# A four-layer decoder on one core: order of the first layers' softmax, of the last context keys and of the first 32-head queries

## Chip, core and metric

The kernel runs on one NeuronCore of a Trainium2 chip as a single program. The metric is the device time of one execution, in microseconds (us); lower is better. All work is in that one launch: eight sub-layers, one after another, on 1024 rows of 512 values.

## What is computed

`x` is (16, 64, 512) and is handled as 1024 rows in 8 tiles of 128 rows. `ctx` is a context of the same shape. Each of four layers adds a cross attention and a feed-forward to `x`:

```
x = x + L0_xattn(layernorm(x), ctx)   # 8 heads, a window of 16 places along the 512 columns, rows as channels
x = x + L0_ffn(layernorm(x))          # int8 fake-quantised gate, up, down; silu; clip
x = x + L1_xattn(layernorm(x), ctx)   # 32 query heads, 8 key heads of 128, keys and queries RMS-normed
x = x + L1_ffn(layernorm(x))          # mxfp4 fake-quantised weight and input
x = x + L2_xattn(layernorm(x), ctx, ctx)  # 32 query heads of 16
x = x + L2_ffn(layernorm(x))          # 16 of 64 low-rank experts per row
x = x + L3_xattn(layernorm(x), ctx)   # 16 query heads of 96
x = x + L3_ffn(layernorm(x))          # 3-bit weight
```

In L0, every place of the 512 columns attends to 16 neighbouring places: the scores of a tile are 16 x 16 x 512 values, a softmax over the 16, and a weighted sum of 16 shifted copies of the values. In L1 the keys and values come from `concat([context, latents])`, so half of them depend on the context alone and can be made before L0 is done.

## The kernel before

**Two lanes on one instruction stream.** Every sub-layer is a Python generator that issues instructions and yields an estimated cost of what it has issued. `merged` (L1840) runs two of them: `main` and `side`. After each step of `main`, with cost c, it advances `side` until the costs that `side` has yielded reach `rate` x c. `side` marks its progress with `MARK`; `main` asks for it with `Need(n, rate)`: `merged` then advances `side` alone, with nothing of `main` between, until more than n marks have come, and goes on with the new rate. TensorE (PE) takes its instructions exactly in the order in which they are traced (`tc.manual_schedule(engines={PE})`, L1975). The other engines and the SyncE queue (SP), which issues all DMAs, are ordered by the framework's scheduler from trace order and its own estimates; `behind_main` and `issue_after` pin a DVE instruction behind the last DVE instruction that `main` has traced.

**What runs when.** `side` does L0 for the four groups of two tiles each (window attention, then the int8 feed-forward), and yields a `MARK` after each group's feed-forward. After that it does L1_ffn to the end of the decoder for the first four tiles. `main` does L1's attention: first the context keys and values of all 32 units (4 pairs of key heads x 8 tiles), then for each group of two tiles 8 key heads x 2 tiles, and afterwards L1_ffn to the end for the last four tiles.

**Window attention** (`WindowAttention`, L231). `__init__` loads its weights `w4` and biases `bcol`; `context` loads a context tile `cn`; `normed` makes the layernorm; `keys_values` and `queries` make the padded keys `kp`, values `vp` and `qs` (PE tiles ps_kv0 and ps_q0, line L323); `dots` multiplies shifted keys with queries on DVE (`prod`, L371), sums over the head's rows on PE (L392), copies the result to `dots`, and turns it with a round trip through DRAM (`dots_d`, L402 and L404). `softmax` (L409) works on two halves of a tile: maximum and subtraction on DVE (L420, L421), exponential on ACT (L422), sum and reciprocal on DVE (L426, L427), product on GpSimd (POOL, L428), and yields 1.5 after the exponential and 1.5 after the product, so 6 in all for a tile. The weights go to DRAM (`att_d`, L431) and come back spread out (`att`, `load`, L443: four buffers). `output` (L448) multiplies them with the values on DVE (`pv`, L468, pinned behind main's last DVE instruction) and adds the products up on POOL (`acc`, L478): 16 steps, each of two products and two additions. `project` multiplies with the output weights on PE (L323).

**Int8 feed-forward** (`Int8Ffn`, L515). Its weights come through a staging tile `room` of 128 x 1024 in three parts: `load` (L538, SP) and `split` (L546 on ACT and L547 on POOL: a high part and the rest). `load(n+1)` overwrites `room` and so waits for `split(n)`. `load_rows` (L556) then loads six rows of scales, spread over all partitions, into `rv` (128 x 2304). `steps` runs a tile through norm, scale, turn, hidden (PE ps_gu, L615), gated, limited, turn_hidden, down (PE ps_dn, L652; `y` L660, `x` L661), and then `normed.norm` and `normed.turn` make the next layernorm of the tile and transpose it (PE ps_xT, copied on ACT L178) into `kvT`, from which L1 makes its queries.

**Context keys in L1** (`normed_attention`, L752). `context_keys` multiplies a context tile with the weights of a key-head pair (PE ps_ckv, L812; 16 matmuls), copies the result on ACT (`ckv`, L821), squares it (`csq`, L823) and makes the RMS factor `r` (DVE L801, L802; POOL L125). Two units later `context_scale` multiplies the keys by it (`ckn`, L831, in the two buffers of tag `qn`), and four units later `context_turn` transposes them (PE ps_ckT), scales the copy (ACT L837) and saves keys and values to DRAM (`s`, L839). The costs are 3.4, 0.0 and 0.3. All 32 units finish, with the four turns that trail, before `Need(2, 0.85)` and the first queries:

```
        pair_weights(0)
        yield Need(1, 0.95)
        yield from ticks(
            [(hp, t) for hp in range(NKV // 2) for ts in groups for t in ts],
            [(4, context_turn, 0.3), (2, context_scale, 0.0), (0, context_keys, 3.4)],
        )
```

**The units of L1's attention** follow: per unit `queries` (PE ps_q, L860, and the loads of the saved `kT` and `v`; `v` has six buffers), `keys_values` (PE ps_kv, L878), `scale`, `turn`, `scores`, `turn_weights`, `values`, `project` with costs that add up to 11.4; a group has 16 units.

**Block sums** (`block_sums`, L1234). For L2_ffn and L3_xattn the weights are combined once on POOL (L1258, four subtractions for each of 14 parts, two buffers) and stored to DRAM (`sums_d`, L1247). They are traced while `side` is in `small_head_attention`, one subtraction after four out of five of its steps; `store(n - 1)` is traced in the third subtraction of part n.

## Time and profile before

| what | value |
|---|---|
| median of 3 runs | 1616.03 us (1613.99 to 1616.12) |
| the profiled execution | 1613.3 us, of which the span is 1611.5 us |
| PE (matmuls) busy | 1552.4 us, 96% of the span |
| DVE, POOL, ACT busy | 1006.4, 629.2, 624.9 us |
| DMA | 226.49 MB, mean 141 GB/s |

Two rows of the page show the span in 40 slices of 40.3 us, in tenths:

```profile
PE   7899899999999999999999999999999999999999
...
PEclk9999899999999999999999999999999999999999
DMA  7992349623694346954436932214211005231031
```

How to read it: a digit 9 means 90% or more. PE is below that in the first slice, in the second to third and in the fifth; there the granted clock of TensorE is lower, too. DMA is near its full share in the second and third slice. In the views by instruction, a line has the start, the time, the engine with its line, operation and tiles, how many there are, and in brackets the engine's idle time before it with what ended that.

### The profile page before, as it was taken

To read this page: it belongs to the slowest core of one execution; us is meant where nothing else is said; L and a number is where in the kernel's file an instruction comes from. 1 tells how busy PE (TensorE), PEld (TensorE's weight loads), DVE (VectorE), ACT (ScalarE), POOL (GpSimd) and SP (SyncE) were. 2 spreads that over 40 slices of the span, in tenths; PEclk is the share of its full clock that TensorE was granted. 3 is DMA by queue.
4 is the path that set the end of the run, shared out by engine and by line. 5 is a ranking of instruction groups with operands and counts; after the bars stand their busy time and mean duration, and the time that the engine had idled before them with its cause. 6 is when DMAs were issued, how large, how long until landed. Compare 5 with 4: busy or idle time off the path is not lost.

```text
span 1611.5 us, 21995 instructions
## 1 busy us (share of the span) xinstructions
PE 1552.4 (96%) x7446; PEld 976.8 (61%) x7446; DVE 1006.4 (62%) x2133; ACT 624.9 (39%) x1951; POOL 629.2 (39%) x666
## 2 busy tenths in 40 slices
PE   7899899999999999999999999999999999999999
PEld 2234456565555655566665566577666688866886
DVE  7687488676697566777954265358535564822445
ACT  3333444334443444344443354321235533213451
POOL 2394237632385313853325643234113233311232
PEclk9999899999999999999999999999999999999999
DMA  7992349623694346954436932214211005231031
GB/s 235 275 282 89 113 140 283 194 88 119 188 277 135 119 140 179 260 171 175 157 133 213 319 136 74 98 46 179 96 46 47 1 27 190 57 119 41 24 118 40
DMA packets 108703, 226.49 MB, mean 141 GB/s; under 512 B 50096, under 2 KB 67632, under 8 KB 97968
## 3 DMA queue, kind: packets, MB, share of 16 engines
q1 hardware_dynamic: 108592, 225.09, 44.3%
q8 instruction: 60, 0.98, 0.2%
q14 instruction: 51, 0.42, 0.1%
HBM read 198.32 MB, written 26.74 MB: 140 GB/s over the span
## 4 chain that ended last, share of the span: by engine, by line
PE 70%; DVE 12%; DMA 7%; POOL 4%; ACT 3%; issue 3%; SPq 0%; ACTq 0%; POOLq 0%; DVEq 0%
PE ps_wo L746 9%; PE ps_q L860 9%; PE ps_q L1674 5%; PE ps_kv L878 5%; PE ps_s L696 4%; PE ps_wo L1285 4%; PE ps_a L737 4%; PE ps_ckv L812 3%; PE ps_pT L143 3%; PE ps_k L1658 3%; PE ps_v L1616 3%; PE ps_h L1285 3%; DMA sums_d<-sums 2%; PE ps_o L1285 2%; DMA att<-att_d 2%
## 5 line engine op out<-in xcount | busy, mean ns | idle before, releaser
L746 PE MATMUL ps_wo<-l1a_o,aT 128*128 128x512 f32 x512 | 232.9, 598 | 3.3 <-ACT aT L930 3.1
L860 PE MATMUL ps_q<-l1a_w,kvT 128*128 128x512 f32 x512 | 232.7, 597 | 0.0
L712 ACT ACTIVATE p<-ps_s,mx 128x128 f32<-128x128 f32 x384 | 135.7, 370 | 218.2 <-DVE mx L707 195.1
L721 POOL TENSOR_TENSOR p<-p,sm 128x512 f32<-128x512 f32 x96 | 104.0, 1084 | 238.3 <-DVE sm L720 210.6
L125 POOL TENSOR_TENSOR r<-r,mhalf 128x5 f32<-128x5 f32 (+1 forms) x96 | 102.0, 1062 | 216.3 <-DVE r L802 213.1
L860 PEld LDWEIGHTS ps_q<-l1a_w,kvT 128*128 128x128 f32 x512 | 96.2, 191 | 116.6 <-issue 115.0
L746 PEld LDWEIGHTS ps_wo<-l1a_o,aT 128*128 128x128 f32 x512 | 93.2, 192 | 101.3 <-issue 96.3
L878 PE MATMUL ps_kv<-l1a_w,kvT 128*128 128x256 f32 x512 | 122.3, 382 | 2.4 <-DVE x L159 2.4
L478 POOL TENSOR_TENSOR acc<-acc,pv 128x512 f32<-128x512 f32 x96 | 122.1, 1296 | 3.7 <-DVE pv L468 3.0
L812 PE MATMUL ps_ckv<-l1a_kv,kvT 128*64 128x512 f32 x512 | 116.9, 598 | 5.1 <-ACT ckv L821 5.1
L801 DVE TENSOR_REDUCE r<-sq 128x5 f32<-128x640 f32 x64 | 52.2, 816 | 101.2 <-ACT sq L886 101.1
L878 PEld LDWEIGHTS ps_kv<-l1a_w,kvT 128*128 128x128 f32 x512 | 92.5, 190 | 17.8 <-DVE x L159 3.8
L125 POOL TENSOR_TENSOR rs<-rs,mhalf 128x1 f32<-128x1 f32 x64 | 37.9, 601 | 153.1 <-DVE rs L134 142.8
L868 ACT ACTIVATE sq<-ps_q 128x512 f32<-128x512 f32 x64 | 38.3, 598 | 152.3 <-PE ps_q L860 152.3
L468 DVE TENSOR_TENSOR pv<-att,ps_v 128x512 f32<-128x512 f32 x128 | 82.0, 676 | 23.1 <-DMA att<-att_d 20.8
L696 PE MATMUL ps_s<-kT,qT 128*128 128x128 f32 (+1 forms) x704 | 91.7, 276 | 0.1
L371 DVE TENSOR_TENSOR prod<-qs,kp 128x1024 f32<-128x1024 f32 x64 | 80.8, 1300 | 13.8 <-ACT qs L352 6.9
L159 DVE TENSOR_TENSOR x<-x,ps_wo 128x512 f32<-128x512 f32 x76 | 51.3, 675 | 57.5 <-PE ps_wo L1206 35.1
L696 PEld LDWEIGHTS ps_s<-kT,qT 128*128 128x128 f32 (+1 forms) x704 | 85.1, 192 | 2.5 <-issue 0.9
L1674 PE MATMUL ps_q<-kvT,l3a_w 128*128 128x256 f32 x384 | 85.5, 379 | 0.0
L728 DVE COPY pT<-ps_pT 128x512 f32<-128x512 f32 x96 | 64.3, 681 | 28.9 <-PE ps_pT L143 28.8
L712 ACT ACTIVATION_READ_ACCUMULATOR p<-ps_s,mx 128x1 f32 x384 | 79.9, 208 | 0.0
(231 smaller groups left out, 2968.1 us busy)
## 6 DMA issues: line engine op xcount, KB each, us to landing
l1a_w<-in_l1a_w SPq DMA_DIRECT2D x32, 1536.0 KB, 7.2
att<-att_d SPq DMA_DIRECT2D x64, 512.0 KB, 8.8
l1a_o<-in_l1a_w SPq DMA_DIRECT2D x32, 1024.0 KB, 5.3
w_sums<-sums_d SPq DMA_DIRECT2D x28, 512.0 KB, 5.5
w_sums<-in_sums_w SPq DMA_DIRECT2D x28, 384.0 KB, 4.4
s<-ckv SPq DMA_DIRECT2D x32, 256.0 KB, 4.7
raw<-in_sums_w SPq DMA_DIRECT2D x14, 512.0 KB, 4.6
sums_d<-sums SPq DMA_DIRECT2D x14, 512.0 KB, 5.9
```

The lines of the kernel that those rows point to most:

```text
L125: self.nc.gpsimd.tensor_tensor(out, v, self.k.mhalf[:, : v.shape[1]], ALU.pow)
L468: nc.vector.tensor_tensor(pv.rearrange("p (q w n) -> p q w n", w=2, n=L), att[:, a, :].rearrange("p (q w n) -> p q w n", w=2, n=L), spaced ...
L478: nc.gpsimd.tensor_tensor(sums, before, pv, ALU.add)
L696: nc.tensor.matmul(ps[:, i, :], lhsT=qT[:, i // 2, 2 * (i % 2) : 2 * (i % 2) + 2, :].rearrange("p g s -> p (g s)"), rhs=kTs[i // 2], start ...
L712: nc.scalar.activation(p[:, i, :], ps[:, i, :], AF.Exp, bias=mx[:, i : i + 1], scale=self.scale, accum_out=sm[:, i : i + 1],)
L721: nc.gpsimd.tensor_tensor(p, p, bc(sm, 2, P), ALU.mult)
L746: self.nc.tensor.matmul(ps, lhsT=a, rhs=wo[:, g, :], start=g == 0, stop=g == len(chunks) - 1)
L812: nc.tensor.matmul(ps[j * S : (j + 1) * S], lhsT=k.context(c, 2 * t + 1 - j), rhs=w_pair[hp][:, c, :], start=c == 0, stop=c == NC - 1,)
L860: nc.tensor.matmul(ps, lhsT=k.stream(c, t), rhs=w_qkv[n][0][:, c, :], start=c == 0, stop=c == NC - 1,)
L878: nc.tensor.matmul(ps, lhsT=k.stream(c, t), rhs=w_qkv[n][1][:, c, :], start=c == 0, stop=c == NC - 1,)
L1285: self.ln.nc.tensor.matmul(ps[:, i % 2], lhsT=a(e), rhs=w[:, b * W2 : (b + 1) * W2], start=e == 0, stop=e == len(self.rhs) - 1,)
L1674: nc.tensor.matmul(ps[:, j], lhsT=wq[:, c, (j0 + j) * P : (j0 + j + 1) * P], rhs=k.kvT[:, c, t : t + 2, 1:3, :], start=c == 0, stop=c == N ...
```

## The change

The diff does these things:

- `w4`, `bcol` and the context tiles 0 and 1 are loaded from ACT's queue and no longer from SP's.
- `softmax` is cut into `shifted` (maximum, subtraction), `raised` (exponential) and `divided` (sum, reciprocal, product). The exponential of a half is traced one step after its subtraction, together with the other half's `shifted`. The yields are 3.0, 3.0, 1.5 and 1.5: 9 for a tile.
- `room` is now the first 1024 columns of `rv`, so `load_rows` waits for the last `split`.
- For the first group `Int8Ffn` is run with `last_apart`: the second tile's `normed.turn` is left out of the list of steps. The `MARK` comes at the end of `steps`, and after it a yield of 4.0, the second tile's turn and a yield of 1.0.
- `context_scale` puts `ckn` into tag `v` (six buffers).
- The context steps run, at rate 1.08 in place of 0.95, until the last `context_keys` and one step more. The five steps that remain are taken by `rest(2)` at the end of each `queries` and `keys_values`.
- The rates of the four groups are 0.9, 0.815, 0.815, 0.775 in place of 0.85, 0.78, 0.78, 0.74.
- `block_sums` traces `store(n - 1)` in the second subtraction, and is advanced by one step for every 1.4 of cost that `small_head_attention` yields.

```diff
@@ WindowAttention.__init__
-        nc.sync.dma_start(self.w4, wt)
+        nc.scalar.dma_start(self.w4, wt)
...
-        nc.sync.dma_start(self.bcol, bias)
+        nc.scalar.dma_start(self.bcol, bias)
@@ WindowAttention.context
-        self.ln.nc.sync.dma_start(cn, self.ctx_in[t * P : (t + 1) * P, :])
+        queue = self.ln.nc.scalar if t < 2 else self.ln.nc.sync
+        queue.dma_start(cn, self.ctx_in[t * P : (t + 1) * P, :])
@@ WindowAttention.softmax
-        for c in range(2):
-            part = e[:, :, c * n_at_once : (c + 1) * n_at_once]
-            by_place = part.rearrange("p w n -> p n w")
+        parts = [e[:, :, c * n_at_once : (c + 1) * n_at_once] for c in range(2)]
+
+        def shifted(part):
             mx = ln.small.tile([P, n_at_once], F32, tag="mx0", name="mx0")
             with ln.behind_main():
-                nc.vector.tensor_reduce(mx, by_place, AX.X, ALU.max)
+                nc.vector.tensor_reduce(mx, part.rearrange("p w n -> p n w"), AX.X, ALU.max)
                 nc.vector.tensor_tensor(part, part, bc(mx, 1, WIN), ALU.subtract)
+
+        def raised(part):
             nc.scalar.activation(part, part, AF.Exp, scale=8.0**-0.5)
-            yield 1.5
+
+        def divided(part):
             sm = ln.small.tile([P, n_at_once], F32, tag="sm0", name="sm0")
             with ln.behind_main():
-                nc.vector.tensor_reduce(sm, by_place, AX.X, ALU.add)
+                nc.vector.tensor_reduce(sm, part.rearrange("p w n -> p n w"), AX.X, ALU.add)
                 nc.vector.reciprocal(sm, sm)
             nc.gpsimd.tensor_tensor(part, part, bc(sm, 1, WIN), ALU.mult)
-            yield 1.5
+
+        shifted(parts[0])
+        yield 3.0
+        raised(parts[0])
+        shifted(parts[1])
+        yield 3.0
+        raised(parts[1])
+        divided(parts[0])
+        yield 1.5
+        divided(parts[1])
+        yield 1.5
@@ Int8Ffn.__init__
-        self.room = pool.tile([P, 1024], F32, tag="room", name="room")
         self.rv = pool.tile([P, sum(r.shape[0] for r in rows)], F32, tag="rv", name="rv")
+        self.room = self.rv[:, 0:1024]
@@ Int8Ffn.steps
+        def turn_out(t):
+            if not (last_apart and t == tiles[-1]):
+                normed.turn(t)
...
-                (6, normed.turn, 1.0),
+                (6, turn_out, 1.0),
...
+        yield MARK
+        if last_apart:
+            yield 4.0
+            normed.turn(tiles[-1])
+            yield 1.0
@@ normed_attention
-            kn = pool.tile([P, G, HD], F32, tag="qn", name="ckn")[:, 0:2, :]
+            kn = pool.tile([P, 2, HD], F32, tag="v", name="ckn", bufs=6)
...
+            rest(2)
...
-        yield Need(1, 0.95)
-        yield from ticks(
-            [(hp, t) for hp in range(NKV // 2) for ts in groups for t in ts],
+        yield Need(1, 1.08)
+        units = [(hp, t) for hp in range(NKV // 2) for ts in groups for t in ts]
+        context = ticks(
+            units,
             [(4, context_turn, 0.3), (2, context_scale, 0.0), (0, context_keys, 3.4)],
         )
+        while units[-1] not in kept:
+            yield next(context)
+        yield next(context)
+
+        def rest(n):
+            for _ in range(n):
+                next(context, None)
@@ block_sums
-            if out == 2:
+            if out == 1:
                 store(n - 1)
@@ first_layers
-                yield from ffn.run(tiles)
-                yield MARK
+                yield from ffn.run(tiles, n == 0)
@@ side
-            for n, cost in enumerate(small_head_attention(b, halves[0], i["l2a_w"], weights)):
-                if n % 5 < 4:
+            spent = 0.0
+            for cost in small_head_attention(b, halves[0], i["l2a_w"], weights):
+                spent += cost
+                while spent > 1.4:
                     next(sums, None)
+                    spent -= 1.4
@@ main
-            a, groups, [0.85, 0.78, 0.78, 0.74], i["l1a_w"], i["l1a_kv"], i["l1a_n"]
+            a, groups, [0.9, 0.815, 0.815, 0.775], i["l1a_w"], i["l1a_kv"], i["l1a_n"]
```

More of the change, by code (lines that the diff above doesn't have):

```diff
@@ L558, in load_rows, with run, steps @@
             at += n
-    def run(self, tiles):
+    def run(self, tiles, last_apart=False):
         with ExitStack() as es:
-            yield from self.steps(tiles, self.ln.pool(es, "l0f"))
-    def steps(self, tiles, pool):
+            yield from self.steps(tiles, self.ln.pool(es, "l0f"), last_apart)
+    def steps(self, tiles, pool, last_apart):
         ln, k, nc = self.ln, self.ln.k, self.ln.nc
@@ L894, in keys_values @@
             d.update(kn=kn, r=r)
+            rest(2)
         def scale(u):
```

## The prediction

> **What bounds it now.** I read the busy time by stage first. PE is busy in 1552 of 1611.5 us, so nearly everything is paced by the order in which PE gets its work, and an edit that adds or removes no matmul can only win or lose PE's gaps and its slow clock. Columns: PE, PEld, DVE, ACT, POOL busy, granted clock, DMA share, GB/s.
>
> ```profile
> 40.00:80.00 40.00, 35.77 (x164) 11.35 (x162) 26.70 (x47) 14.52 (x32) 15.71 (x16) 1.00 0.91 273
> 80.00:120.00 40.00, 39.16 (x180) 12.45 (x178) 33.63 (x54) 11.45 (x28) 36.58 (x33) 1.00 1.00 282
> 120.00:160.00 40.00, 38.96 (x210) 16.17 (x208) 31.03 (x76) 15.31 (x34) 19.73 (x24) 1.00 0.29 96
> 160.00:200.00 40.00, 32.90 (x136) 16.76 (x134) 19.38 (x44) 16.24 (x43) 10.75 (x21) 0.83 0.32 114
> 200.00:240.00 40.00, 40.00 (x191) 22.44 (x188) 34.43 (x50) 19.31 (x65) 13.39 (x10) 1.00 0.44 136
> ```
>
> The reader should see the two stages where PE is short (40 to 80, 160 to 200), the clock of 0.83, and that between them POOL (36.6 of 40) and DMA (1.00) are full. PE's timeline names the gaps:
>
> ```profile
> 6.60 3.38 PE L323 MATMUL ps_kv<-cn,w 64*64 64x512 f32 x16 [6.60 <-DMA cn<-in_ctx]
> ...
> 55.28 3.65 PE L812 MATMUL ps_ckv<-l1a_kv,kvT 128*64 128x512 f32 x16 [1.41 <-ACT ckv L821]
> ...
> 60.73 3.65 PE L812 MATMUL ps_ckv<-l1a_kv,kvT 128*64 128x512 f32 x16 [1.42 <-ACT ckv L821]
> ...
> 66.15 3.65 PE L812 MATMUL ps_ckv<-l1a_kv,kvT 128*64 128x512 f32 x16 [1.40 <-ACT ckv L821]
> ...
> 126.06 1.95 PE L323 MATMUL ps_o<-acc,w 64*64 64x512 f32 x16
> ...
> 166.56 0.66 PE L143 MATMUL ps_ckT<-ident,ckn 128*128 128x128 f32 x2 [2.12 <-DVE r L802]
> ...
> 176.22 1.11 PE L143 MATMUL ps_xT<-ident,xn 128*128 128x128 f32 x4 [4.59 <-DVE rs L134]
> 177.12 5.14 PE L860 MATMUL ps_q<-l1a_w,kvT 128*128 128x512 f32 x8
> ...
> 183.82 3.60 PE L860 MATMUL ps_q<-l1a_w,kvT 128*128 128x512 f32 x8
> ```
>
> Why ACT is late three times is on its own timeline: the exponential (L422) stands first in its queue and waits 3.65 us for the subtraction, and the copy that empties PE's bank stands behind it.
>
> ```profile
> 54.13 0.63 ACT L422 ACTIVATE dots<-dots 128x512 f32<-128x512 f32 x1 [3.65 <-DVE dots L421]
> 54.66 0.57 ACT L821 COPY ckv<-ps_ckv 128x512 f32<-128x512 f32 x1
> ```
>
> Last come POOL's chain of additions, which ends 0.3 us before the output projection at 126.06, and later, among all waits, POOL's for the stored block sums:
>
> ```profile
> 74.26 1.53 POOL L478 TENSOR_TENSOR acc<-pv 128x512 f32<-128x512 f32 x1 [1.02 <-DVE pv L468]
> ...
> 124.49 1.27 POOL L478 TENSOR_TENSOR acc<-acc,pv 128x512 f32<-128x512 f32 x1
> ```
> ```profile
> POOL sums L1258 <- DMA sums_d<-sums: 18.4, 11, 2.7
> ```
>
> **The change, part by part.** Times are against the profiled execution, 1613.3 us.
>
> *Start.* Four issues leave SP: w4 0.42, bcol 0.43, two cn 0.91, together 1.76 us (SP's timeline); ACT issues them at about the same price, and is idle to 5.88. What stands behind them on SP comes as much earlier. The first matmul waits for cn, so the gain lies between 0 (DMA share is 1.08 from 4 to 8 us, the engines may be the limit) and 1.76; I take the middle, **-0.9**. [...] No run here shows two queues yet.
>
> *Exponentials.* With a step between subtraction and exponential the copy no longer stands behind a wait: 1.41 + 1.42 + 1.40 = **-4.2** (bounds 0, if the scheduler orders ACT as before, and -4.2).
>
> *Order.* Costs give where PE meets the first projection. Before, 15 (dots) + 12 (softmax) + 8 + 43.5 (output) + 5.5 = 84 of side's cost lie between the second mark and it, and main's n-th context unit has supplied 0.95 x (3.4n + 0.3(n-4)): the projection follows unit 25. After, it is 90 against 1.08 times the same: unit 23. Units follow each other in 3.96 us (70.10, 74.06). PE is therefore there at 126.06 - 0.9 - 4.2 - 2 x 3.96 = 113.0. The two units aren't lost; they now fill the feed-forward behind it.
>
> *What is late next: POOL's additions.* The first pv stands behind the r of unit 11 (72.22, then 72.30), so it moves with PE by 5.1, and the first addition from 74.3 to 69.2. From there POOL has 28 additions of 1.32 and 12 r of 0.70: 45.4 us, an end at 114.6 if POOL never waits. If the stage keeps its length (125.8 - 74.3 = 51.5, because DMA is full) it ends at 120.7. I take 116.5, two us of waiting, nearer to POOL's own rows because the first weights are stored some 7 us earlier (two halves no longer cost 5.4 us each), which moves the first loads into a stretch where DMA had room (share 0.48 from 52 to 56). The wait at the projection is **+3.5** (bounds +1.6 and +7.7). Waits of about 2 us have cost a slow clock in one place (322 to 330, granted 0.79, 1.7 us lost) and not in another (514 to 522, 2.89 us of waiting, 1.00): **+0.9**, between 0 and 1.7. [...]
>
> *The end of the first group.* Side's cost to the third mark was 124 against a supply of 112.5, so 9 to 11 units ran with nothing of main between; now 130 against 1.08 x 117.5 = 126.9, about 3. From one tile's down to its transposed layernorm takes 5.45 us (170.77 to 176.22). In the new order PE has, after the first tile's down, 2 context units, the other tile's down and three short transposes, 9.6 us; after the second's down one unit, the first's turn, the first queries and keys (3.44 + 1.73) and three short transposes, some 10.8. Both cover 5.45; without that cover the 4.59 is back. Gone are 2.12 + 0.30 + 4.59 = 7.0 and the slow clock: down 2.07 for 1.20, two xT 0.45 each, the first queries 5.14 for 3.60, 3.3 in all. New is a wait of the first queries for the first tile's copy, 0.6 as such a wait costs at 881 (0.67). **-9.7**, bounds -10.3 and -5.
>
> *Moved without a price.* The five trailing context steps are the same matmuls, copies and three stores on SP (some 0.4 each), taken between the first queries; kT and v of those heads are needed six heads later. ckn in six buffers rather than two removes a DVE wait (2.42 at 42.13) that PE does not see. The row loads of rv wait for the last split (POOL, to 46.96; they went at 40.71): on SP, stores and att loads stand behind them. The rows are first read at 132; SP may be held 6 us, hidden as long as the second tile's dots still load before their new turn, at most 2.5 us on the additions, in the bounds above.
>
> *Groups two to four.* The same counting of costs puts their projections where they were (distance from first stored weights within 1.2 us). The wait of 0.59 at 246.83, behind an exponential, goes: **-0.6**. Between turn and hidden two tiles lose their filler: about 4.4 us each (a wait of 2.06 now, at 323.59, with 2.3 of filler), against 2.06 + 2.89 today, so 3.9 more if nothing else gives; I take **+2.0** (0 to +5.6, with a slow clock).
>
> *Block sums.* 61 steps over 85.7 of cost, instead of bunched between 857 and 932. PE waits there at 924.72, 926.61 and 930.23 (1.81 + 1.15 + 1.62 = 4.58), behind an r of POOL that stands behind those sums. Earlier stores have three steps to land. **-3.5**, bounds -4.6 and +3: the moved subtractions (0.73 each) could delay POOL where it is idle now.
>
> *Rates.* Main's four groups supply 182.4 x (3.305 - 3.15) = 28.3 more, side has 23 more: it ends some 5 units ahead, and main's tail alone is 5 longer. That tail has 4.7 us of gaps in its last 112: 0, within 2.
>
> Sum: -0.9 - 4.2 + 3.5 + 0.9 - 9.7 - 0.6 + 2.0 - 3.5 = **-12.5**. The profiled execution lies 2.7 under the median shown, so 1616.0 - 12.5 = **1603.5 us**.
>
> **Rivals.**
> 1. *DMA holds the output stage at its length* (share 1.00 from 80 to 120 speaks for it, POOL's 92% against): a wait of 7.7 with a slow clock, +4.2 + 0.8 on the sum, -7.5: 1608.5. Chance 0.20.
> 2. *Nothing comes back*: no wait at the projection, none added at hidden, all of the sums: -0.9 - 4.2 - 9.7 - 0.6 - 4.6 = -20: 1596. The full POOL speaks against. 0.12.
> 3. *It doesn't do what it says.* Only PE's order is fixed; if the scheduler places exponentials and sums as before, the 4.2 stays, PE reaches the projection at 117.2 and waits to 124.9 with a slow clock: -0.9 + 7.7 + 1.7 - 9.7 + 2 = +0.8: 1617. The explicit step of cost speaks against. 0.11.
> 4. *Slower: SP is held by the row loads.* They wait for the last split, which stands on ACT and POOL among exponentials and products; att_d and att stand behind. From the store (57.87) to the first pv are 14.4 us, 2 to the first addition, then 51.5: with SP released at T the additions end at T + 68. All gain is gone when that is 128 (113 + 15 of savings), T = 60, and each us beyond costs one; at T = 65, 1621. The split ended at 46.96 and would have to slip by 13. 0.09.
>
> **Numbers.** My forecast has 0.48. Range 1594 to 1614: it takes in rivals 1 and 2 and the forecast's own bounds, and leaves out the tails and most of 3 and 4. About 0.2%, 3.2 us, is what a measurement of this kernel tells from no change: faster (under 1612.8) 0.80, same 0.09, slower 0.11.
>
> **What would show it.** Right: no bracket at ps_ckv with ACT ckv between 50 and 70; a bracket with POOL acc at the first projection, near 113, of 2 to 5 us; first queries near 166 at 3.6; clock 1.00 where 0.60 was (165 to 182); sums spread to about 1030. Wrong: a gap at the projection of 8 or more, first row loads holding SP past 50 with att behind, new brackets at ps_gu over 4, or POOL r waits new between 940 and 1040.

## The result and the profile after

| | before | after |
|---|---|---|
| median, measured together | 1616.07 us (1611.72 to 1623.32, 8 runs) | 1627.9 us (1621.44 to 1631.54, 8 runs) |
| profiled execution, its span | 1613.3, 1611.5 us | 1627.3, 1625.5 us |
| PE busy in it | 1552.4 us | 1556.5 us |
| first 32-head queries (ps_q) at | 177.12 us | 173.34 us |
| queries of unit 56, of unit 58 at | 919.32, 950.35 us | 919.85, 963.17 us |

The ratio of the times, after to before, is 1.0066 (95%: 1.0041 to 1.0091): slower by 0.7%, where 12.5 us less was forecast, and outside the range. Units are counted from 0. Of the 14 us by which the profiled executions differ, 12.3 arise between unit 56 and unit 58 of L1's attention (43.3 us for two units, before 31.0).

The busy time by stage of the changed kernel, columns as in the prediction's first table, and below them the row of the kernel before for 900 to 950:

```profile
40.00:80.00 40.00, 40.00 (x184) 12.73 (x184) 26.53 (x54) 16.04 (x35) 19.33 (x19) 1.00 0.96 290
80.00:120.00 40.00, 37.20 (x168) 11.54 (x164) 34.21 (x54) 12.42 (x29) 37.48 (x35) 1.00 0.86 267
120.00:160.00 40.00, 36.73 (x182) 16.08 (x184) 28.81 (x70) 12.22 (x26) 14.00 (x18) 0.91 0.19 66
160.00:200.00 40.00, 37.88 (x174) 19.68 (x171) 19.31 (x45) 19.12 (x51) 11.65 (x22) 1.00 0.40 137
900.00:950.00 50.00, 37.08 (x187) 21.12 (x186) 13.54 (x27) 12.64 (x40) 32.78 (x44) 0.90 0.85 282
...
900.00:950.00 50.00, 45.27 (x288) 26.88 (x287) 28.00 (x61) 20.64 (x63) 30.79 (x38) 1.00 0.74 266
```

The two stages that were short, 40 to 80 and 160 to 200, are repaired: PE is busy 40.00 us for 35.77 and 37.88 for 32.90, and the second has a clock of 1.00 for 0.83 (it is the fifth slice of the page of before, the only one there with a lower clock digit). But the stages between have lost 4.2 of the 9.2 that these won (80 to 160: 73.9, before 78.1), and 900 to 950 is new: PE 37.08 (before 45.27) at a granted clock of 0.90 (before 1.00). PE's timeline names the waits:

```profile
116.13 1.07 PE L324 MATMUL ps_o<-acc,w 64*64 64x512 f32 x2
121.06 3.56 PE L324 MATMUL ps_o<-acc,w 64*64 64x512 f32 x14 [3.85 <-POOL acc L492]
...
134.74 1.97 PE L143 MATMUL ps_q<-ident,xs 128*128 128x128 f32 x8 [2.21 <-DVE xs L597]
...
949.13 1.09 PE L143 MATMUL ps_qT<-ident,qn 128*128 128x128 f32 x4 [12.92 <-DVE sm L1208]
```

The 12.92 us are put down to the last DVE instruction to end before the matmul (`sm`). But PE's transpose reads `qn`. On DVE that stands just ahead, and waits for POOL:

```profile
928.96 0.17 DVE L825 TENSOR_SCALAR r<-r 128x5 f32<-128x5 f32 x1
...
948.29 0.69 DVE L926 TENSOR_TENSOR qn<-qn,r 128x512 f32<-128x512 f32 x1 [17.01 <-POOL r L125]
```

And this is POOL in those 18 us:

```profile
928.35 1.42 POOL L1292 TENSOR_TENSOR sums<-raw 128x256 f32<-128x256 f32 x2 [3.52 <-DMA sums_d<-sums]
929.72 1.54 POOL L1292 TENSOR_TENSOR sums<-raw,sums 128x256 f32<-128x256 f32 x2
934.78 1.41 POOL L1292 TENSOR_TENSOR sums<-raw 128x256 f32<-128x256 f32 x2 [3.52 <-DMA sums_d<-sums]
936.15 1.52 POOL L1292 TENSOR_TENSOR sums<-raw,sums 128x256 f32<-128x256 f32 x2
937.63 1.41 POOL L1292 TENSOR_TENSOR sums<-raw 128x256 f32<-128x256 f32 x2
939.00 1.52 POOL L1292 TENSOR_TENSOR sums<-raw,sums 128x256 f32<-128x256 f32 x2
943.25 1.41 POOL L1292 TENSOR_TENSOR sums<-raw 128x256 f32<-128x256 f32 x2 [2.73 <-DMA sums_d<-sums]
944.61 1.52 POOL L1292 TENSOR_TENSOR sums<-raw,sums 128x256 f32<-128x256 f32 x2
946.09 1.04 POOL L1209 TENSOR_TENSOR p<-p,sm 128x512 f32<-128x512 f32 x1
947.09 1.17 POOL L125 TENSOR_TENSOR r<-r,mhalf 128x5 f32<-128x5 f32 x1
```

The input of `r` is ready at 929.1. POOL's queue has four parts of block sums ahead of it, 16 subtractions of 0.7 us, and three of the parts wait for a stored part to leave its buffer (3.52, 3.52, 2.73; the first of these waits is over before 929.1). `r`, needed by PE, runs 18 us after it could. The sums were not spread to 1030 as forecast; the last ends at 946. They stand in one heap, as before, only a worse one. In the kernel before, `r` came behind the heap, too, but PE waited less for it:

```profile
921.19 1.53 POOL L1258 TENSOR_TENSOR sums<-raw,sums 128x256 f32<-128x256 f32 x2
922.68 1.17 POOL L125 TENSOR_TENSOR r<-r,mhalf 128x5 f32<-128x5 f32 x1
...
923.88 0.69 DVE L901 TENSOR_TENSOR qn<-qn,r 128x512 f32<-128x512 f32 x1 [5.84 <-POOL r L125]
...
924.72 0.63 PE L143 MATMUL ps_qT<-ident,qn 128*128 128x128 f32 x4 [1.81 <-DVE qn L901]
```

### The profile page after: what moved, and what is told of

Same layout as the page of the kernel before. It is cut to its first block, busy times and chain, and to the rows that moved or that the text cites. A ratio compares the mean times of both kernels' runs of the same rounds, so it can differ in the third digit from the quotient of the medians.

```text
span 1625.5 us, 21983 instructions
## 1 busy us (share of the span) xinstructions
PE 1556.5 (96%) x7442; PEld 979.6 (60%) x7446; DVE 1014.7 (62%) x2133; ACT 626.8 (39%) x1951; POOL 629.0 (39%) x666
## 4 chain that ended last, share of the span: by engine, by line
PE 74%; DVE 12%; DMA 6%; POOL 3%; ACT 2%; issue 2%; ACTq 0%; SPq 0%; DVEq 0%; POOLq 0%
PE ps_wo L769 10%; PE ps_q L883 10%; PE ps_kv L902 6%; PE ps_q L1708 5%; PE ps_s L719 4%; PE ps_a L760 4%; PE ps_wo L1319 4%; DMA att<-att_d 3%; PE ps_pT L143 3%; PE ps_ckv L835 3%; PE ps_v L1650 3%; PE ps_k L1692 3%; PE ps_h L1319 2%; PE ps_wo L1240 2%; PE ps_q L1172 2%; PE ps_o L1616 2%
## 5 line engine op out<-in xcount | busy, mean ns | idle before, releaser
L902 PE MATMUL ps_kv<-l1a_w,kvT 128*128 128x256 f32 x512 | 127.3, 393 | 5.3 <-DVE x L159 4.7
```

Source lines behind the costliest of these rows:

```text
L902: nc.tensor.matmul(ps, lhsT=k.stream(c, t), rhs=w_qkv[n][1][:, c, :], start=c == 0, stop=c == NC - 1,)
```

## The experiments

Each was timed in five rounds against the kernel before. The ratio to before is of the times; waits and positions are from one profiled execution of each, which lies up to 7 us off that kernel's median (the kernel before with both edits of the sums: 1612.6, median 1619.5).

**Which part of the block sums it was.** Four kernels. *Both edits of the sums undone:*

```diff
-            if out == 1:
+            if out == 2:
...
-            spent = 0.0
-            for cost in small_head_attention(b, halves[0], i["l2a_w"], weights):
-                spent += cost
-                while spent > 1.4:
+            for n, cost in enumerate(small_head_attention(b, halves[0], i["l2a_w"], weights)):
+                if n % 5 < 4:
                     next(sums, None)
-                    spent -= 1.4
```

> The changed kernel with the two edits of the block sums undone (one subtraction after four of five steps, store in the third subtraction). The changed kernel has one PE gap of 12.9 us at 949.13 behind an r of POOL that stands behind sums; before, there were 4.6 us of gaps at 924 to 931. H1, the edits of the sums put four parts of sums ahead of main's r: the gap falls back to 3 to 6 us, the granted clock from 900 to 950 back to 1.00, and the time is 11 to 15 below the changed kernel's 1627.9, so 1613 to 1617. H2, the shift of main against side by the new rates and the longer softmax makes the coincidence, whatever the pacing: the gap stays at 8 or more and the time above 1622. H3, the edits of the first layer cost the time: the first queries come later than 173 and the time stays above 1622 though the gap is gone.

*The kernel before with both edits alone* (the same diff the other way round):

> The kernel before with the two edits of the block sums alone. H1: a gap of 8 or more behind an r of POOL between 920 and 960, and 1624 to 1632 (8 to 15 over 1616.1). H2, the edits are harmless by themselves and only meet main's r at the new rates: gaps of 5 or less there and 1614 to 1618. My forecast's step, that the sums are spread to about 1030 and the gaps go: 1612 to 1613.

*The changed kernel, with POOL's order pinned* (`merged` keeps main's last POOL instruction as it does the last one on DVE):

```diff
-            nc.gpsimd.tensor_tensor(t[out], v, w, ALU.subtract)
+            with ln.behind_main_pool():
+                nc.gpsimd.tensor_tensor(t[out], v, w, ALU.subtract)
@@
+    def behind_main_pool(self):
+        last = self.k.last_pool_of_main
+        return self.tc.issue_after(last) if last is not None else ExitStack()
```

> The changed kernel, with every subtraction of the block sums held behind the last POOL instruction that main has traced, so that POOL takes them in traced order relative to main's r. H1 and its mechanism (POOL's order is the scheduler's own, and it takes sums ahead of the r that is traced earlier): no PE gap over 3 us between 900 and 1000, clock 1.00, sums spread from about 880 to 1030, and 1611 to 1616. H2: POOL is simply too full there and the delay returns at another r: 1620 or more.

*The pacing alone undone* (the second hunk of the first diff), the earlier store kept:

> The changed kernel with the old pacing of the block sums (one subtraction after four of five steps), but the new place of the store (second subtraction). With both edits undone the two units from 919 on took 34.4 us, with both kept 43.3, with the sums pinned 25.9, and the times were 1.0020, 1.0066 and 0.9975 of before. If the pacing made the loss, the two units take 33 to 36 us and the ratio is 1.001 to 1.003; if the earlier store made it, 41 or more and 1.005 or more.

With the kernel before and the pin (further below), they make a table; the time for two units runs from the queries of unit 56 to those of unit 58:

| kernel | two units, us | ratio to before (95%) |
|---|---|---|
| before | 31.0 | 1 |
| before, both edits of the sums | 33.4 | 1.0017 (0.9998 to 1.0036) |
| after | 43.3 | 1.0066 (1.0041 to 1.0091) |
| after, both undone | 34.4 | 1.0020 (1.0005 to 1.0035) |
| after, pacing undone | 33.8 | 1.0020 (1.0000 to 1.0040) |
| after, sums pinned | 25.9 | 0.9975 (0.9952 to 0.9997) |
| before, sums pinned | 25.3 | 0.9964 (0.9947 to 0.9981) |

The pinned kernel's POOL takes the sums in between main's work:

```profile
928.19 1.17 POOL L126 TENSOR_TENSOR r<-r,mhalf 128x5 f32<-128x5 f32 x1
929.33 0.72 POOL L1299 TENSOR_TENSOR sums<-raw,sums 128x256 f32<-128x256 f32 x1
930.01 1.17 POOL L1299 TENSOR_TENSOR sums<-raw 128x256 f32<-128x256 f32 x1
931.14 1.04 POOL L1215 TENSOR_TENSOR p<-p,sm 128x512 f32<-128x512 f32 x1
```

and its stage has no gap and no slow clock:

```profile
900.00:950.00 50.00, 50.00 (x309) 30.49 (x308) 28.46 (x57) 23.02 (x68) 26.12 (x31) 1.00 0.67 234
```

So the mechanism is shown: the loss is POOL's order, which is not that of the trace, and holding each subtraction behind main's last POOL instruction removes all of it (43.3 to 25.9 us; 1611.3 against a before of 1615.9). The heap costs the two units 5.7 us before (31.0 against 25.3) and 17.4 after. The pacing makes the larger part of the difference, the earlier store none that can be seen. My expectation that the old sums alone would give back 13 us failed: they gave back some 7 (1.0066 to 1.0020), because main's r and the heap still meet (4.25 us of waiting there and 1.18 at the next matmul; with the pacing alone undone 3.80 and 0.97). On the kernel before, the new edits cost 2.4 us in the two units, in the changed kernel 8.9. So the loss seems to need both, the pacing and the shifted lanes. That rests on one profiled execution of each: in the times the two effects are 2.7 and 7.4 us, and their difference lies within its uncertainty.

**What the rest of the change is worth.** *The kernel before, with the pin alone:*

> The kernel before, with every subtraction of the block sums held behind main's last traced POOL instruction, and nothing else. The changed kernel with the same pin ran in 1611.3. T1, the pin alone makes that time and the rest of the change nets nothing: the three gaps of before at 924 to 931 (4.6 us) go, and 1609.5 to 1612.5. T2, the pin only repairs what the new pacing broke, and the edits of the first layers are worth the 4 to 5 us by which the first queries come earlier: 1614.5 to 1617.

0.9964, against 0.9975 for the changed kernel with the pin: the rest of the change nets +0.0011, with an uncertainty of about 0.0028, or +2 us give or take 4.5. By the ratios T1 is right. Where it goes is seen in PE's idle time by stage (us, from the windows, stage less PE busy):

| kernel | 0-40 | 40-80 | 80-200 | 200-700 | 700-900 | 900-1000 | 1000-1500 |
|---|---|---|---|---|---|---|---|
| before | 8.9 | 4.2 | 9.0 | 12.7 | 3.0 | 5.4 | 11.7 |
| before, pin | 8.6 | 4.2 | 8.5 | 15.5 | 3.2 | 0.7 | 12.5 |
| after | 9.2 | 0.0 | 8.2 | 11.6 | 7.4 | 14.3 | 14.2 |
| after, pin | 9.7 | 0.0 | 9.0 | 10.3 | 7.5 | 0.7 | 14.5 |
| after, pin, old exponentials | 9.7 | 0.0 | 7.1 | 14.0 | 7.4 | 0.7 | 13.7 |
| after, pin, old end | 9.1 | 0.4 | 15.1 | 10.1 | 3.7 | 0.4 | 25.7 |
| after, pin, rates halfway | 9.5 | 0.0 | 9.5 | 12.7 | 6.8 | 1.1 | 23.3 |
| before, pin, new rates | 9.2 | 5.0 | 8.1 | 22.4 | 2.9 | 1.0 | 22.8 |
| before, pin, new end, rates 0.01 up | 9.0 | 3.8 | 8.0 | 12.6 | 1.4 | 0.1 | 25.2 |
| after, pin, both edits at the projection | 9.1 | 0.6 | 5.6 | 11.3 | 7.0 | 0.7 | 13.6 |

**The exponentials.** The old order, at the new costs:

```diff
+        for c in range(2):
...
+            nc.scalar.activation(part, part, AF.Exp, scale=8.0**-0.5)
+            yield 3.0
...
+            nc.gpsimd.tensor_tensor(part, part, bc(sm, 1, WIN), ALU.mult)
+            yield 1.5
```

> The changed kernel with the pinned sums, and the old order inside the softmax: each half's exponential directly behind its subtraction, with costs 3.0 and 1.5 for a half, so that the sum of a tile stays 9 and PE's order the same. My forecast's term: three waits of ps_ckv for ACT's ckv of 1.4 us come back between 50 and 70, and the time is 4.2 over that of the changed kernel with pinned sums, 1615.5. Rival: the additions of POOL set when the first projection runs (121 us), and whatever PE gains before, it waits there (3.8 us): the waits come back, the wait at the projection shrinks by as much, the first queries move by less than 1.5 us and the time by less than 1.5: 1610 to 1613.

1608.1, ratio 0.9943 (0.9925 to 0.9962): 5 us under the same kernel with the new order, with 5 us of uncertainty, and no row shows where they would come from (the two profiled executions are 1609.0 and 1608.8). Neither side of the expectation was right, for in this execution the three waits did not come back at all. ACT in that kernel:

```profile
52.03 0.63 ACT L429 ACTIVATE dots<-dots 128x512 f32<-128x512 f32 x1 [2.59 <-DVE dots L428]
52.57 0.57 ACT L837 COPY ckv<-ps_ckv 128x512 f32<-128x512 f32 x1
...
57.51 0.63 ACT L429 ACTIVATE dots<-dots 128x512 f32<-128x512 f32 x1 [3.69 <-DVE dots L428]
58.05 0.57 ACT L837 COPY ckv<-ps_ckv 128x512 f32<-128x512 f32 x1
...
62.97 0.63 ACT L429 ACTIVATE dots<-dots 128x512 f32<-128x512 f32 x1 [3.68 <-DVE dots L428]
63.51 0.57 ACT L837 COPY ckv<-ps_ckv 128x512 f32<-128x512 f32 x1
64.65 0.58 ACT L837 COPY ckv<-ps_ckv 128x512 f32<-128x512 f32 x1
```

The copies still stand behind the exponential's wait, and PE has no wait. A round with an exponential takes 5.5 us where PE's unit takes 3.96, so each puts ACT some 1.5 us further behind; the copy is 0.5 late at 52.57 and 3.5 at 63.51, and the second copy at 64.65 catches up. Copies up to 3.5 late left PE without a wait here. Before, the copy at 49.23 was 3.6 late already, and PE was held from 55.28 on for three rounds running.

In other kernels with the old order and the new costs, further below, a part of these waits is there, at most in the one whose first loads are on SP's queue (0.62 and then):

```profile
64.60 3.65 PE L827 MATMUL ps_ckv<-l1a_kv,kvT 128*64 128x512 f32 x16 [1.43 <-ACT ckv L836]
```

Before, PE's waits behind an exponential there add up to 4.23 us; with the old order at the new costs they are 0 to 2.05 in six kernels, and with the new order 0 to 0.82 in seven. So the step between subtraction and exponential is worth little of the 4.2. The larger part is where costs and rate together put the exponentials among main's units; no run has one without the other (old order, old costs and a rate of 1.03 leave 1.12). The step also costs: the first addition on POOL starts at 74.48 in the changed kernel, and at 72.09 and 72.21 in two kernels that have the new costs and the new end with the old order.

**The start.** *Old sums, SP's queue* and *pinned sums, old exponentials, SP's queue*:

```diff
-        nc.scalar.dma_start(self.w4, wt)
+        nc.sync.dma_start(self.w4, wt)
```

(and so for bcol and the context tiles)

> As the first of these kernels (old block sums), and with w4, bcol and the context tiles 0 and 1 loaded from SP's queue again. In the changed kernel the first matmul starts at 6.69 (before 6.60) and the first statistics of x at 4.51 (before 3.41). H1, the second queue only lets the context tiles' transfers take the place of x's: the first matmul stays within 0.2 of 6.6, x's first statistics fall back to about 3.4, the first queries come 0.5 to 1.5 earlier than in the first of these kernels, and the time is 0.5 to 1.5 lower. H2, my forecast's term: the time is 0.9 higher. H3: no difference, within 0.3.

> The same base (ratio 0.994), with w4, bcol and the context tiles 0 and 1 on SP's queue again. My forecast's start term: first matmul some 0.9 later and ratio 0.0006 higher. Theory from the executions so far (first matmul at 6.7 to 7.1 with ACT's queue in six kernels, 6.2 to 7.4 without in four): the second queue gains nothing, first matmul at 6.2 to 6.9, first statistics of x near 3.4 in place of 4.5, and a ratio of 0.992 to 0.995.

1.0026 (1.0009 to 1.0043) against 1.0020, and 0.9952 (0.9930 to 0.9974) against 0.9943. Both differences have the sign and about the size of the forecast's 0.9 us (0.0006), but lie inside uncertainties of 0.0023 and 0.0029: no gain is shown, and one of 0.9 is not excluded. The first matmul begins, over the profiled executions, at 6.7 to 7.1 with ACT's queue and at 6.2 to 7.4 without. What the two queues do shift is x: its first statistics on DVE start at 4.51 to 4.61 with ACT's queue (three profiles) and at 3.41 and 3.44 without (two), so about 1 us later.

**The end of the first group.** Undone in the changed kernel with the pin, and done without the change's other parts in the kernel before with the pin (there with rates of its own: 1.03 for the context, then 0.86, 0.79, 0.79, 0.75):

```diff
-            rest(2)
...
-        yield Need(1, 1.08)
+        yield Need(1, 0.95)
...
-        while units[-1] not in kept:
...
-                yield from ffn.run(tiles, n == 0)
+                yield from ffn.run(tiles, False)
```

> The changed kernel with the pinned sums, and the old end of the first group: no turn kept apart, all context keys and turns before the first queries, rate 0.95. My forecast's term of 9.7 for this part, less the 2.6 to 4.4 that the wait at the projection took back: the gaps of 2.1 and 4.6 and the slow clock between 160 and 182 come back, first queries at 175 to 178 instead of 171.7, and 1615 to 1620. Rival T1, that what is gained before the first queries is lost again at the later feed-forwards: first queries late as above, but the time within 1.5 of 1611.3.

> The kernel before with the pinned sums and the new end of the first group alone: second tile's turn apart, the last context steps between the first queries, ckn in six buffers; rate 1.03 for the context, and 0.86, 0.79, 0.79, 0.75 behind it, a little over the old ones. The old exponentials and costs, SP for all loads. My forecast's term for this part: no gaps of 2.1 and 4.6 and no slow clock between 160 and 182, less a wait of 3 to 5 at the first projection, which comes two units earlier: first queries 4 to 7 before 176.7, and as much off the ratio of 0.996, so 0.992 to 0.994. Rival, all of it is given back by waits behind it: first queries as early, ratio 0.995 or more.

Undone: first queries at 185.24 in place of 171.66, and 160 to 200 has 11.1 us of idle and a granted clock of 0.74. Of the 13.6 us, 8 are a later projection (129.8 for 121.7), which the lower rate brings with the longer costs. Done on the kernel before: first queries at 174.57 (before, pin: 176.70), and 34.8 us of idle up to 1000 in place of 40.7. Up to there it is a gain. But both kernels are slow, 1.0095 (1.0068 to 1.0121) and 1.0061 (1.0042 to 1.0080), and both have 25 us of idle from 1000 to 1500, where main and side are in the last layers.

**The rates.** Halfway back in the changed kernel with the pin (0.88, 0.80, 0.80, 0.76), the new ones in the kernel before with the pin, and a little up from the new ones (0.91, 0.82, 0.82, 0.78) on the version with the old exponentials:

```diff
-            a, groups, [0.9, 0.815, 0.815, 0.775], i["l1a_w"], i["l1a_kv"], i["l1a_n"]
+            a, groups, [0.88, 0.80, 0.80, 0.76], i["l1a_w"], i["l1a_kv"], i["l1a_n"]
```

> The changed kernel with the pinned sums and rates of 0.88, 0.80, 0.80, 0.76 for the four groups, about halfway back to the old ones. In the changed kernel with pinned sums PE has gaps of 5.9 us between 700 and 800 (before 1.1). T3, the higher rates bunch the third and fourth group's feed-forward and cost those 4 to 5 us: the gaps fall below 3.5 there and the time by 1.5 to 4, to 1607 to 1610. My forecast's step (rates worth 0 within 2): 1610 to 1613.

> The kernel before with the pinned sums and the changed kernel's rates 0.9, 0.815, 0.815, 0.775, nothing else. The kernel before with the pin alone has 1.1 us of PE gaps from 700 to 800, the changed kernel with the pin 5.9. T3, the rates make that gap, because side takes more steps for each of main's and so has fewer of main's matmuls between its own: 4 us or more of gaps there, and 2 to 6 over the kernel before with the pin (1613.1 beside a before of 1617.6, ratio 0.996), so a ratio of 0.998 to 1.000, more if the last layers meet badly, too. My forecast's step, rates worth 0 within 2: a ratio of 0.995 to 0.998.

> The same base (ratio 0.994), with rates 0.91, 0.82, 0.82, 0.78 in place of 0.9, 0.815, 0.815, 0.775, so side 0.6 to 1.1 per cent further ahead. Theory: what main and side do at the same time in the last layers is set by rates and costs together, and where it is moved the waits behind 1000 us change by more than what is gained before: idle of PE from 1000 to 1500 other than 13.7 by 4 us or more, either way, and a ratio off 0.994 by 0.003 or more. Rival: only big moves do that (0.02 to 0.05 in a rate cost 20 us): ratio 0.992 to 0.996.

1.0085 (1.0058 to 1.0112), 1.0137 (1.0101 to 1.0173), and 0.9977 (0.9951 to 1.0003). The first two are far above both expectations. Between 700 and 800, where T3 put the cost, the idle with the new rates alone is 2.5 (T3: 4 or more), so T3's place is wrong; but a change of 0.015 to 0.02 in the rates costs 18 us, and one of 0.035 to 0.05 without the costs that belong to it 28. The largest rise in idle is in 1000 to 1500 again (to 23 us, by 8.8 and 10.3). It makes 9 of the 17 and 10 of the 26 us between the profiled executions; the rest is idle in other stages and a longer busy time of PE. The kernel with rates halfway and the one with the new end have the same waits there, shown from the first:

```profile
1124.57 6.57 PE L1326 MATMUL ps_o<-w_sums,sh 128*128 128x256 f32 x16 [4.25 <-DVE sh L1513]
...
1239.11 1.45 PE L1231 MATMUL ps_a<-pT,vbd 128*32 128x256 f32 x10 [2.59 <-ACT pT L1223]
...
1420.22 1.71 PE L144 MATMUL ps_xT<-ident,xn 128*128 128x128 f32 x8 [4.74 <-DVE xn L137]
```

and from the other:

```profile
1124.79 5.98 PE L1312 MATMUL ps_o<-w_sums,sh 128*128 128x256 f32 x16 [4.26 <-DVE sh L1499]
...
1238.73 1.91 PE L1217 MATMUL ps_a<-pT,vbd 128*32 128x256 f32 x10 [2.58 <-ACT pT L1209]
...
1419.76 1.97 PE L144 MATMUL ps_xT<-ident,xn 128*128 128x128 f32 x8 [4.75 <-DVE xn L137]
```

These are the same instructions at the same times, so one and the same meeting of the lanes, reached from two kernels by different edits; of the three waits the changed kernel with the pin has only the last (3.84), the kernel before with the pin none. That it is set by how far side is ahead of main is the likely reading; no run varies that alone. By it, the change kept the distance by raising costs and rates together. The slight step up gave 17.1 us of idle there for 13.7, and 5.5 us of time, with an uncertainty of 5.

**What holds the first projection.** On the changed kernel with the pin and the old exponentials. First, *POOL relieved of four additions:*

```diff
+                    if pairs and g == n_groups - 1:
+                        with ln.behind_main():
+                            nc.vector.tensor_tensor(pv, held[a], pv, ALU.add)
+                    if not (pairs and g == n_groups - 2):
-                    nc.gpsimd.tensor_tensor(sums, before, pv, ALU.add)
+                        nc.gpsimd.tensor_tensor(sums, before, pv, ALU.add)
```

> The changed kernel with pinned sums and the old order of the exponentials (1608.1 beside a before of 1617.6, ratio 0.994). Here, in the first group only, the last two products of a half are added to each other on DVE, so that POOL has 24 additions in place of 28, 5.3 us less; DVE gets four additions of some 0.7. Theory, POOL's additions alone set the first projection, and what PE gains before it is lost there: POOL ends near 115 in place of 120.2, the wait at the projection falls from 3.97 to under 1, its matmuls from 3.68 to about 2, the first queries come 4 to 5.5 earlier, and the ratio is 0.991 to 0.992. Rival, DVE or the loads of att hold the stage at its length: the additions end at 118 or later and the wait stays over 2.

Then *one more context unit ahead of the projection*, alone, and both together:

```diff
-            yield 4.0 + self.pause / 4
+            yield 4.0 + self.pause / 4 + 3.7 * (tiles[0] == 0)
```

> The changed kernel with pinned sums and the old order of the exponentials (ratio to before 0.994), with 3.7 more of cost in front of the first group's projection, so that one more context unit of PE comes before it and one less behind it. Taking 5.3 us of additions from POOL left the additions' end at 119.9 and the wait at 3.64. Theory now: the last products stand on DVE behind the last context unit traced before them, so PE at the projection always waits for the round from that unit's matmuls over ACT's copy, DVE, POOL's r and back, some 4 us, unless another unit stands between. The wait then falls from 3.97 to under 1, its matmuls from 3.68 to 1.9, the additions still end near 120, the first queries come 2 to 5.5 earlier and the ratio is 0.991 to 0.993. Rival, the additions move back with the unit and the wait stays over 2: ratio 0.994 or more.

> Both edits of the first group together, on the changed kernel with pinned sums and the old order of the exponentials: the last two products of a half added on DVE, and one more context unit in front of the first projection. Alone they gave 0.9939 and 0.9940 beside 0.9943 without them. In every kernel so far the first queries come 49.5 to 52.3 us after the last addition on POOL. If that chain of side sets the first queries, they come at 50 plus or minus 1 after the additions' end here, too, wherever PE waits in between, and the ratio stays within 0.992 to 0.996. If PE's wait at the projection is what costs, the wait is under 1 and the first queries come before 168, ratio under 0.992.

0.9939 (0.9918 to 0.9961), 0.9940 (0.9918 to 0.9962), and together 0.9919 (0.9894 to 0.9944), 1602.4 beside a before of 1614.7. With fewer additions alone POOL is busy 39.6 us from 70 to 120 in place of 44.2, and its additions end at 120.0 in place of 120.3; the wait stays:

```profile
120.05 3.46 PE L331 MATMUL ps_o<-acc,w 64*64 64x512 f32 x14 [3.64 <-POOL acc L490]
```

DVE's timeline has the reason. The last products are pinned behind main's `ckn` and `r` of the last units, and these wait for POOL's `r`:

```profile
110.54 1.49 DVE L853 TENSOR_TENSOR ckn<-ckv,r 128x256 f32<-128x256 f32 x1 [0.72 <-POOL r L126]
...
115.68 1.07 DVE L824 TENSOR_SCALAR r<-r 128x2 f32<-128x2 f32 x1
116.67 0.67 DVE L476 TENSOR_TENSOR pv<-att,ps_v 128x512 f32<-128x512 f32 x1
...
117.91 0.68 DVE L488 TENSOR_TENSOR pv<-pv 128x512 f32<-128x512 f32 x1
```

With the later projection alone the wait there falls to 0.96 and its matmuls to 1.94, as expected, but the additions end 3.2 later (123.4) and the first transposes then wait 3.88; the first queries come at 172.94, no earlier than 171.16. Only both together remove the wait at the projection and bring the first queries to 167.30:

```profile
118.80 2.47 PE L331 MATMUL ps_o<-acc,w 64*64 64x512 f32 x16
...
132.28 1.09 PE L144 MATMUL ps_q<-ident,xs 128*128 128x128 f32 x8 [3.09 <-DVE xs L596]
...
167.30 3.70 PE L882 MATMUL ps_q<-l1a_w,kvT 128*128 128x512 f32 x8 [0.68 <-ACT kvT L184]
```

That is the second case of the last expectation. POOL, DVE's pinned order and PE lie within 4 us of each other there, and relieving one alone gives nothing that can be seen. In time, the step from 0.9943 to 0.9919 is 4 us with an uncertainty of 5, so the gain of the two edits is seen in the positions only. This version, which has the pin too, beats both kernels: 0.8% under before, 1.5% under the change.

## Why the prediction was wrong, point by point

- **Block sums, -3.5 "instead of bunched": the step that failed.** Measured +12.3 in the two units concerned (43.3 us for 31.0; 25.9 with POOL's order held). The forecast itself says that only PE's order is fixed, then took the trace's spacing of the subtractions as POOL's order; POOL ran 16 of them, with two waits for stores, ahead of main's r. Its upper bound of +3 priced moved subtractions at 0.73 each; it had no case for such a heap. Its list of signs of being wrong did name this one, new waits behind POOL's r between 940 and 1040.
- **Exponentials, -4.2.** The three waits went (40 to 80: PE 40.00), but mostly by where costs and rate put the exponentials; the delayed exponential itself brings 0 to 2 us there and holds back the first addition by some 2.3. The size is right, the mechanism mostly not: luck.
- **Start, -0.9.** Not seen: first matmul at 6.69, before 6.60, x's statistics 1.1 later (4.51 for 3.41), and no difference in time beyond its uncertainty. ACT issued the four loads in 1.85 us (0.40, 0.46, 0.99), SP before in 1.76, and from issue to landing x's tiles took 4.0 us (median; before 2.7), the context tiles 5.3 (before 4.0).
- **Order: PE at the projection at 113.0.** It was there at 116.1, behind unit 23 as reckoned, and after two of the 16 matmuls it waits from 117.2. Units followed at 3.96 as reckoned, but the unit that began at 38.0 before begins at 41.3: the first dots are later by 0.8, and the 64 matmuls of dots ahead of it take 12.5 us for 10.3, some of them at the pace of DVE's products:

```profile
14.11 4.91 PE L393 MATMUL ps_dot<-prod,group 128*32 128x512 f32 x16 [2.14 <-DVE prod L372]
...
39.98 1.05 PE L393 MATMUL ps_dot<-prod,group 128*32 128x512 f32 x4 [0.38 <-DVE prod L372]
41.33 1.08 PE L835 MATMUL ps_ckv<-l1a_kv,kvT 128*64 128x512 f32 x4
```

- **POOL's additions: first at 69.2, end at 116.5, wait +3.5 and clock +0.9.** First at 74.5 (before 74.3), end at 121.0. Of the 5.3 us by which the first addition is late, the later units make 3.3, the delayed exponential about the rest. The wait measured 3.85, its matmuls 3.56, against 1.94 where the wait was 0.96. The size of the wait is right because PE came 3 us late and the additions 4.5, which is luck, and its cause is DVE's pinned order as much as POOL. The clock was low behind the wait: 0.91 granted from 120 to 160 (1.00 before, without that wait), and the 1.6 lost (3.56 for 1.94) are nearer to the upper bound of 1.7 than to the 0.9 taken. The wait's length alone does not tell: in other kernels here the 14 matmuls took 3.39 after a wait of 2.46 (the new end on the kernel before) and 2.76 after one of 3.79 (the changed kernel with the pin).
- **End of the first group, -9.7.** The mechanism is right: the gaps of 2.12 and 4.59 and the slow clock are gone, and undone, gaps and a slow clock are back in that stage, with first queries 13.6 later, 8 of them from the later projection. The gain at the first queries is only 3.8, since the projection ran 4.6 us late (121.1 for 116.5) and PE waited again behind it (2.21 at 134.74).
- **Groups two to four, +1.4.** The idle from 200 to 900 rose by 3.3, most of it at the fourth group's transposes and hidden matmuls (700 to 800: 5.4, before 1.1). From 700 to 900 neither the new rates alone (2.9) nor the new end with its own rates (1.4) has it; no run separates its cause.
- **Rates, 0 within 2.** About right for this change, with +2.6 of idle from 1000 to 1500, but for no reason the forecast gave: the rates moved by themselves cost 18 and 28 us, the new end without the change's costs and rates 16.
- In sum, 26.5 us lie between the forecast and the profiled execution: 16 in the block sums (12.3 where -3.5 stood), 6.6 ahead of the first queries (3.8 where 10.4 stood), the rest in the two items before this one.
- The rivals: none of the four was the case. The third is nearest in mechanism, for it too says that only PE's order is fixed; but it left the sums as before and lost the exponentials' 4.2. The row loads of rv were issued by 48.3, so the one for slower, SP held, was wrong in its mechanism, too.

## What to carry to other kernels

Where a framework orders an engine by itself, the trace's spacing of work is no schedule: look on that engine for what stands ahead of the instruction PE waits for, and pin the filler behind the main lane's last instruction there. Here that one pin was worth more than all the reordering of the first layers. Price a rate between two lanes together with the costs it divides, and look at every later stage where the lanes meet.

## What was not expected of the hardware

An engine's order can cost more than its load: POOL with 4.6 us less to do in 50 ended 0.3 us earlier. And the clock was low where the waits were: in the two stages of the changed kernel with waits of 3.85 and 12.92 us (120 to 160, 900 to 950) the granted clock was 0.91 and 0.90, and where the pin took the second wait away it was 1.00. With three short waits, 1.15 to 1.81 between 924 and 931, it was 1.00 from 900 to 950 before.
